# Cross-attention's query and output products as seven half-block products in place of eight, with the order of four engines written out

## The chip, the cores and the metric

The kernel runs on one core of one Trainium2 chip, in one launch. The metric is the device time in microseconds. The kernel before was run three times; every run also has a time of its own, and one more execution was profiled. Each execution gives the core's span (first to last instruction) and the clock that TensorE was granted, as a share of full speed.

## The reference

A block of a diffusion transformer, all in float32, for 8 batches of 512 rows of width 512, with 16 heads of width 32. `ctx` has 77 rows a batch. Cut to what matters:

```python
# phase x: cross-attention with a modulated layer norm
q = (ada_ln(x) @ Wq + bq)                       # 8 x 512 x 512
k, v = split(ada_ln(ctx) @ Wkv + bkv)           # 8 x 77 x 512 each
x = x + softmax(q k^T / sqrt(32)) v @ Wp + bp   # per head
# phase a: self-attention, gated
x = x + gate_a * (self_attention(modulate(ln(x))) @ W_proj + b_proj)
# phase c: cross-attention with a plain layer norm
q_c = ln(x) @ W_qc + b_qc
k_c, v_c = split(ln(ctx) @ W_kvc + b_kvc)
x = x + softmax(q_c k_c^T / sqrt(32)) v_c @ W_cproj + b_cproj
# phase m: MLP, gated
x = x + gate_m * (gelu(modulate(ln(x)) @ W_mlp1 + b_mlp1) @ W_mlp2 + b_mlp2)
```

## The kernel before

The kernel goes through the phases x, a, c and m one after the other; x between phases lies in DRAM, and a batch of it (four tiles of 128 x 512) is loaded into one of three buffers. `cross_phase` does phases x and c; it is the part that changes.

In `cross_phase` a unit is one batch `b` and one group `fc` of four heads (128 columns of q), 32 units a phase. For a unit:

- `queries(b, fc)` makes q transposed, 128 x 512, from four matmuls over the 128-row blocks of the transposed, normalised x (`mm_T`, line 353); ScalarE takes it out of PSUM with bias and scale (`qT`, line 579).
- `scores(b, fc)` makes 16 small matmuls of 77 columns (line 597) into two PSUM tiles of two heads each (`sc[0]`, `sc[1]`, pool `ps_s`). VectorE takes row maxima (line 606) and subtracts them (608), ScalarE takes the exp of the 128 x 616 block (611), VectorE sums (613), takes reciprocals (614) and multiplies (615). So it does for both tiles.
- `outputs(b, fc, ps)` turns the weights of each of the four heads with four transposes (634); ScalarE copies each turned head out (`pT`, 635); four matmuls against the values follow (639), and VectorE adds a bias (`oT`, 646).
- `project(b, t)` makes one 128 x 512 block of the output projection from four matmuls (`mm_N`, 361); VectorE adds the bias row (`res`, 376), GpSimd adds x (380), and SyncE's queue stores it (381).
- `ln_T` takes the statistics of a batch on VectorE (276, 277), a reciprocal square root by an integer seed and three Newton steps of small operations (288 to 297), normalises (`xh`, 301), and turns the result with 16 transposes (339); ScalarE copies them out (`xnT`).

TensorE alone has a written order in these phases (`manual_schedule(engines={ENG.PE})`); the other engines' orders come from the scheduler. `Filler` is a queue of generators: between the four turns of one unit, `fill.pump()` issues one matmul each of the next unit's query; what is left (the projection of the batch before, layer-norm transposes) is issued by `fill.drain()`. Softmax of a unit runs on VectorE and ScalarE while TensorE turns and multiplies for the unit before it.

PSUM has in these phases two double tiles for scores, two banks with the tag `m` (queries, projection, `o_ps`) and two with the tag `t` (turned heads, layer-norm transposes).

In phase x, `later_modulation(b)` follows a batch's last projection and makes one of six modulation blocks, whose weights it loads itself (`mod_unit`). In phase c, the keys of the last two head groups are put into the `Filler` first (`head`).

The MLP of phase m already uses seven products for eight half blocks (`Quad`, matmuls at line 1214, VectorE additions at 1222, one ScalarE copy at 1229, GELU at 1247).

Of the kernel before, what the change touches and what calls it, by code (L numbers as in the profile page):

```python
# [10 lines left out]
F32 = mybir.dt.float32  # L11
I32 = mybir.dt.int32
AF = mybir.ActivationFunctionType
ALU = mybir.AluOpType
# [11 lines left out]


class Filler:

    def __init__(self):
        self.q = deque()
        self.done = set()
        self.credit = 0.0
        self.left = 0
        self.rate = 0.0

    def add(self, key, gen, n=4):
        self.q.append((key, gen))  # L40
        self.left += n

    def pace(self, slots):

        self.rate = self.left / slots

    def step(self):
        while self.q:
            key, gen = self.q[0]
            try:  # L50
                next(gen)
                self.left -= 1
                return True
            except StopIteration:
                self.done.add(key)
                self.q.popleft()
        return False

    def pump(self):
        self.credit += self.rate  # L60
        while self.credit >= 1.0:
            self.credit -= 1.0
            if not self.step():
                self.credit = 0.0
                return

    def need(self, key):
        while key not in self.done:
            assert self.q, key
            if not self.step():  # L70
                break
        assert key in self.done, key

    def drain(self):
        while self.step():
            pass
# [3 lines left out]
def tile_pixart_block(ctx: ExitStack, tc: tile.TileContext, a: dict, out: bass.AP):  # L80
# [55 lines left out]
    def mod_unit(wname, bname, u, dst, psp, tag, gate=None, plus_one=False):  # L136


        w = load_w(wname, u)
        ps = psp.tile([P, H], F32, tag=tag, name=f"mod_ps_{wname}_{u}")  # L140
        if gate is not None:
            for k in range(KC):
                nc.tensor.matmul(
                    ps[:B, :], lhsT=csT[:, k, :], rhs=w[:, k, :],
                    start=(k == 0), stop=(k == KC - 1),
                )
            b_row = load_row(bname, u, "bv", parts=B)
            nc.vector.tensor_tensor(b_row, ps[:B, :], b_row, ALU.add)
            nc.sync.dma_start(out=gate, in_=b_row)
            return  # L150
# [76 lines left out]
    with tc.tile_pool(name="setup_ps", bufs=2, space=PSUM) as spp:  # L227
# [22 lines left out]
        for name in ("L0_xcond_bq", "L1_xcond_b_qkv", "L1_xcond_b_qc"):  # L250
# [66 lines left out]
    def ln_T(b, eps, nm, pool, psp, res, scale=None, shift=None, bufs=5, tag="t"):  # L317
# [6 lines left out]
        yield  # L324
        mv, y = run(pieces)
        xh = pool.tile([P, NT, H], F32, tag="xh", bufs=1, name=f"xh_{nm}{b}")
        if nm == "c" and b == 0:

# [3 lines left out]
        else:  # L332
            for t in range(NT):
                normalise(xh[:, t, :], xb[:, t, :], mv, y, t, P)
        yield
        for k in range(KC):
# [3 lines left out]
            o = pool.tile([P, N], F32, tag="xnT", bufs=bufs, name=f"xnT_{nm}{b}_{k}")  # L340
            if scale is None:
                nc.scalar.copy(o, pt)
            else:
                nc.scalar.activation(
                    o, pt, AF.Identity, bias=shift[:, k, b : b + 1], scale=scale[:, k, b : b + 1]
                )
            res.append(o)
# [24 lines left out]

    def add_residual(b, t, ps, b_row, gate, pool, nm):

        tmp = pool.tile([P, H], F32, tag="res", bufs=2, name=f"res_{nm}{b}_{t}")
        nc.vector.tensor_tensor(tmp, ps, b_row, ALU.add)  # L376
        xt = x_sb[nm, b][:, t, :]
        if gate is not None:
            nc.gpsimd.tensor_tensor(tmp, tmp, gate, ALU.mult)
        nc.gpsimd.tensor_tensor(xt, xt, tmp, ALU.add)  # L380
        nc.sync.dma_start(out=x_dst[nm][b][ts(t, P), :], in_=xt)
# [33 lines left out]
    with tc.tile_pool(name="ps_s", bufs=2, space=PSUM, reuse_waits="tile") as ps_s:  # L415
# [17 lines left out]
        def context_x(eps, w_k, w_v, bkv, work, prep, cx):  # L433
# [38 lines left out]
            for j in range(KC):  # L472
                for g in range(2):
                    pk = ps_m.tile([P, H], F32, tag="m", name=f"ckT_ps_x{j}_{g}")
                    for k in range(KC):
# [5 lines left out]
                        kT[:, j, ts(g, HB)], pk[:, :HB], AF.Identity, bias=bias_cols(bkv, 1, j)  # L481
# [4 lines left out]
        class ContextC:  # L486
# [62 lines left out]
            def keys(self, j):  # L549
                for at, n, cT in ((0, H, self.cT), (H, RL, self.last)):  # L550
                    pk = ps_m.tile([P, H], F32, tag="m", name=f"ckT_ps_c{j}_{at}")
                    for k in range(KC):
# [7 lines left out]
                        bias=bias_cols(self.bkv, 1, j),  # L560
                    )
                return evac

        def cross_phase(
# [3 lines left out]

            w_q, w_o = w
            bq, bkv, bo_row = names  # L570
            work = stack.enter_context(tc.tile_pool(name=f"work_{nm}", bufs=2, reuse_waits="tile"))
            fill = Filler()
            st = [dict(xT=[], q={}, o=[]) for _ in range(B)]

            def queries(b, fc):
                pq = ps_m.tile([P, H], F32, tag="m", name=f"q_ps_{nm}{b}_{fc}")
                yield from mm_T(pq, w_q, fc, st[b]["xT"])
                qT = work.tile([P, N], F32, tag="qT", bufs=2, name=f"qT_{nm}{b}_{fc}")
                nc.scalar.activation(
                    qT, pq, AF.Identity, bias=bias_cols(bq, 1, fc), scale=SCALE  # L580
                )
                st[b]["q"][fc] = qT

            def project(b, t):
                pr = ps_m.tile([P, H], F32, tag="m", name=f"proj_ps_{nm}{b}_{t}")
                yield from mm_N(pr, w_o, st[b]["o"], ts(t, P))
                add_residual(b, t, pr, bo_row, None, work, nm)
                if t == NT - 1 and between is not None:
                    between(b)

            def scores(b, fc):
                nmf = f"{nm}{b}_{fc}"
                qT = st[b]["q"].pop(fc)
                sc = [ps_s.tile([P, 2, H], F32, tag="s", name=f"s_{nmf}_{i}") for i in range(2)]
                for t in range(NT):
# [808 lines left out]
```

## Time and profile before

| what | value |
|---|---|
| runs | 2602.67 us median of 3 (2601.11 to 2604.31) |
| profiled execution | 2603.28 us, span 2601.4 us, granted clock 0.989 |
| phase x, from the first query (75.4 to 488.3 us) | 412.9 us, TensorE busy 405.1, VectorE 287.2, ScalarE 156.6, GpSimd 40.6 |
| phase a (530 to 1340 us) | 810.0 us, TensorE 752.1, VectorE 658.8, ScalarE 565.6, GpSimd 589.6 |
| phase c, from the first query (1405.1 to 1790.5 us) | 385.4 us, TensorE 381.1, VectorE 286.8, ScalarE 150.8, GpSimd 40.0 |
| phase m (1793 to 2601 us) | 808.0 us, TensorE 792.2, VectorE 442.6, ScalarE 143.9, GpSimd 128.7 |

In what follows, a row of groups by form reads: line, engine, operation, output from inputs, shape, count, then busy time in all, mean length of one in ns, and the idle time of the engine just before them with what ended it. A row of the timeline reads: start, length (both in us), engine, line, operation, count. A row of windows reads: stretch, length, busy time (and count) of TensorE, TensorE's weight loads, VectorE, ScalarE and GpSimd, then the granted clock, the share of DMA time and GB/s. Matmuls overlap, and a float32 matmul has two records of which the second starts before the first ends.

### The profile page before, as it was taken

What the parts mean: (1) busy time and instruction counts of PE and PEld (TensorE: products, weight loads), DVE (VectorE), ACT (ScalarE), POOL (GpSimd) and SP (SyncE); (2) the same over time, 40 slices, a digit from 0 to 9 for tenths busy, and PEclk for the clock granted to TensorE, in tenths of its full rate; (3) what the DMA queues carried; (4) which work ended last, traced back from release to release, by engine and by line L of the source; (5) the groups of instructions that cost most, each with busy time, mean ns of one, the idle gap of its engine ahead of it and who ended that gap; (6) DMA issues with size and microseconds to landing.
All of it is one profiled execution on the core that took longest, in us unless ns stands there. A gap on an engine that the chain in (4) does not pass through costs nothing.

```text
span 2601.4 us, 32647 instructions
## 1 busy us (share of the span) xinstructions
PE 2488.0 (96%) x12517; PEld 1425.3 (55%) x12517; DVE 1744.8 (67%) x3109; ACT 1074.6 (41%) x1471; POOL 848.0 (33%) x692
## 2 busy tenths in 40 slices
PE   7999999989999999999979999998999999999998
PEld 3555554423333333333324555555888888888887
DVE  3676667478787887887784877777655555555553
ACT  1433334366776766767653433432221221221220
POOL 1000000156877768678662011114012012012021
PEclk9999999989999999999989999999999999999999
DMA  7111121279999999999986011113001011011010
GB/s 256 38 54 53 63 72 58 81 147 200 186 195 194 183 194 186 193 203 186 200 180 225 13 57 37 42 53 122 25 30 53 21 33 53 19 35 53 17 37 25
DMA packets 116407, 264.90 MB, mean 102 GB/s; under 512 B 12595, under 2 KB 29059, under 8 KB 116251
## 3 DMA queue, kind: packets, MB, share of 16 engines
q0 software_dynamic: 37152, 134.28, 27.6%
q1 hardware_dynamic: 73157, 116.76, 13.5%
q10 hardware_dynamic: 5941, 11.76, 1.2%
q8 instruction: 99, 1.62, 0.2%
q14 instruction: 58, 0.47, 0.1%
HBM read 226.39 MB, written 36.37 MB: 101 GB/s over the span
## 4 chain that ended last, share of the span: by engine, by line
PE 40%; issue 27%; DMA 12%; DVE 12%; POOL 6%; ACT 2%; POOLq 0%; SPq 0%; ACTq 0%; DVEq 0%
DMA e_a<-mxd_a 9%; PE proj_ps_c L361 4%; PE proj_ps_x L361 4%; PE q_ps_c L353 4%; PE q_ps_x L353 4%; DVE mx_a L836 3%; PE pT_ps_c L634 2%; PE v_ps L361 2%; PE pT_ps_x L634 2%; POOL res_m L1313 2%; PE proj_ps_a L361 2%; DVE sum_a L886 2%; DVE tu_a L847 2%; POOL xr L1314 2%; DVE part_a L848 2%
## 5 line engine op out<-in xcount | busy, mean ns | idle before, releaser
L879 ACT ACTIVATE e_a<-e_a 128x1024 f32<-128x1024 f32 x256 | 262.4, 1056 | 99.4 <-DMA e_a<-mxd_a 98.9
L870 POOL DMA_DIRECT2D e_a<-mxd_a x256 | 248.0, 2049 | 142.7 <-DMA mxd_a<-mxT_a 130.3
L834 ACT COPY e_a<-sT_a 128x1024 f32<-128x1024 f32 x256 | 253.0, 1010 | 91.3 <-DVE mx_a L836 66.0
L1313 POOL TENSOR_TENSOR res_m<-res_m,gate_m 128x256 f32<-128x256 f32 x64 | 52.1, 814 | 665.9 <-DVE res_m L1311 665.9
L1247 ACT ACTIVATE hT<-hT,bcol 128x512 f32<-128x512 f32 x128 | 92.0, 722 | 237.3 <-DVE hT L1222 229.2
L886 POOL TENSOR_TENSOR sum_a<-e_a,e_a 128x1024 f32<-128x1024 f32 x64 | 150.1, 2363 | 121.8 <-ACT e_a L879 121.3
L380 POOL TENSOR_TENSOR x_x<-x_x,res_x 128x512 f32<-128x512 f32 x32 | 40.6, 1270 | 409.9 <-DVE res_x L376 343.1
L886 POOL TENSOR_TENSOR sum_a<-sum_a,e_a 128x1024 f32<-128x1024 f32 x64 | 171.1, 2684 | 2.7 <-ACT e_a L879 2.7
L816 PE MATMUL sT_a<-qT_a,kT_a 32*128 32x512 f32 x1024 | 153.2, 647 | 18.5 <-ACT e_a L834 16.7
L836 DVE TENSOR_TENSOR mx_a<-sT_a,mx_a 128x1024 f32<-128x1024 f32 x128 | 150.3, 1215 | 23.3 <-PE sT_a L816 23.3
L896 PE MATMUL o_ps_a<-e_a,v 128*32 128x512 f32 x1024 | 145.0, 618 | 13.3 <-ACT e_a L879 13.3
L380 POOL TENSOR_TENSOR x_c<-x_c,res_c 128x512 f32<-128x512 f32 x32 | 40.6, 1269 | 346.4 <-DVE res_c L376 289.5
L635 ACT COPY pT_x<-pT_ps_x 77x512 f32<-77x512 f32 x128 | 72.7, 577 | 189.4 <-PE pT_ps_x L634 189.4
L635 ACT COPY pT_c<-pT_ps_c 77x512 f32<-77x512 f32 x128 | 72.7, 577 | 163.4 <-PE pT_ps_c L634 163.4
L353 PE MATMUL q_ps_x<-xnT_x,w_L_xcond_Wq 128*128 128x512 f32 x256 | 132.7, 604 | 0.0
L1214 PE MATMUL q_ps_h<-x_m,w_L_xcond_W_mlp 128*128 128x256 f32 x512 | 131.7, 380 | 0.0
L1214 PE MATMUL q_ps_h<-xT_m,w_L_xcond_W_mlp 128*128 128x256 f32 x512 | 131.4, 379 | 0.0
L914 DVE RECIPROCAL rz_a<-z_ps_a 128x512 f32<-128x512 f32 x32 | 107.4, 3358 | 34.0 <-PE z_ps_a L907 34.0
L353 PE MATMUL q_ps_c<-xnT_c,w_L_xcond_W_qc 128*128 128x512 f32 x256 | 130.1, 594 | 0.0
L836 DVE TENSOR_TENSOR mx_a<-sT_a,e_a 128x1024 f32<-128x1024 f32 x64 | 77.8, 1224 | 77.0 <-PE sT_a L816 39.3
L1214 PE MATMUL q_ps_h<-x_m,w_s 128*128 128x256 f32 x512 | 122.8, 383 | 5.9 <-DVE w_s L1168 4.9
L361 PE MATMUL proj_ps_a<-w_L_xcond_W_proj,oT_a 128*128 128x512 f32 x256 | 117.6, 604 | 9.9 <-ACT xnT_a L739 9.9
(249 smaller groups left out, 5133.0 us busy)
## 6 DMA issues: line engine op xcount, KB each, us to landing
e_a<-mxd_a POOLq DMA_DIRECT2D x256, 512.0 KB, 11.4
xa<-x_x SPq DMA_DIRECT2D x32, 256.0 KB, 2.0
xr_a<-xa SPq DMA_DIRECT2D x32, 256.0 KB, 4.7
xc<-xr_a SPq DMA_DIRECT2D x32, 256.0 KB, 8.3
x_c<-xc SPq DMA_DIRECT2D x8, 1024.0 KB, 7.1
w_L_xcond_W_mlp<-in_L_xcond_W_mlp_dram SPq DMA_DIRECT2D x8, 1024.0 KB, 6.1
xm<-x_c SPq DMA_DIRECT2D x32, 256.0 KB, 2.0
x_m<-xm SPq DMA_DIRECT2D x8, 1024.0 KB, 5.3
```

The source lines that it names most:

```text
L353: nc.tensor.matmul(ps, lhsT=w[:, k, ts(j, P)], rhs=xT[k], start=(k == 0), stop=(k == KC - 1))
L361: nc.tensor.matmul(ps, lhsT=xT[k][:, cols], rhs=w[:, k, :], start=(k == 0), stop=(k == KC - 1))
L635: nc.scalar.copy(pTs[-1][:, h % 2, :], pp[:S, :])
L816: nc.tensor.matmul(sc[h // 2][:, h % 2, :], lhsT=kT[ts(h, HD), ts(k, P)], rhs=qT[ts(h, HD), :], start=True, stop=True,)
L834: nc.scalar.copy(self.e[k][i], sc[i])
L836: nc.vector.tensor_tensor(self.mx[1 - i], sc[1 - i], self.e[0][1 - i] if k == 1 else self.mx[1 - i], ALU.max,)
L870: nc.gpsimd.dma_start(out=self.e[k][i].rearrange("p h n -> p (h n)"), in_=self.mxd[2 * i : 2 * i + 2, :] .rearrange("h n -> (h n)").partit ...
L879: nc.scalar.activation(self.e[k][i], self.e[k][i], AF.Exp)
L886: engine.tensor_tensor(sum_i, self.e[0][i] if k == 1 else sum_i, self.e[k][i], ALU.add)
L896: nc.tensor.matmul(self.po[ts(h, HD), :], lhsT=vt[:, self.fc * P + h * HD : self.fc * P + (h + 1) * HD], rhs=self.e[k][h // 2][:, h % 2, : ...
L914: nc.vector.reciprocal(r, self.pz)
L1214: nc.tensor.matmul(self.banks[n][:, half], lhsT=lhsT, rhs=rhs, start=(k == 0), stop=(k == len(pairs) - 1),)
```

## The change

Queries and the output projection of a batch are 512 x 512 x 512 products. They are now made of quadrants of 256 by the scheme with seven products (that of the MLP) in place of eight. A `Seven` makes half of the columns of all seven products: two 128 x 256 output blocks in each half, so two `Seven`s for a batch's queries and two for its projection. Each of its steps issues one product (two matmuls of 256 columns) and what reads it. Two products share a PSUM bank of tag `m`.

```diff
+        class Seven:
+            ORDER = (1, 2, 6, 7, 5, 4, 3)
+            def steps(self):
+                for n, i in enumerate(self.ORDER):
+                    if n % 2 == 0:
+                        bank = ps_m.tile([P, 2, N2], F32, tag="m", name=f"s{n}_ps_{self.nm}")
+                    ps = bank[:, n % 2]
+                    for k in range(2):
+                        nc.tensor.matmul(
+                            ps, lhsT=self.lhs[i][:, k], rhs=self.rhs[i][:, k],
+                            start=(k == 0), stop=(k == 1),
+                        )
+                    if i == 1:
+                        p1 = self.temp("p1")
+                        self.first(p1, ps)
+                    elif i == 2:
+                        nc.vector.tensor_tensor(self.dst[0, 0], ps, p1, add)
+                    elif i == 6:
+                        u2 = self.temp("u2")
+                        nc.vector.tensor_tensor(u2, ps, p1, add)
+                    elif i == 7:
+                        u3 = self.temp("u3")
+                        self.third(u3, ps, u2)
+                    elif i == 5:
+                        p5 = self.temp("p5")
+                        self.fifth(p5, ps)
+                        nc.gpsimd.tensor_tensor(u2, u2, p5, add)
+                        nc.gpsimd.tensor_tensor(self.dst[1, 1], u3, p5, add)
+                    elif i == 4:
+                        nc.vector.tensor_tensor(self.dst[1, 0], ps, u3, add)
...
+                    else:
+                        nc.vector.tensor_tensor(self.dst[0, 1], ps, u2, add)
...
+                    yield
```

For queries `first` is a ScalarE activation with the bias, for the projection a VectorE addition of the bias row; `fifth` is a ScalarE copy (with one more GpSimd addition for the projection). The sums of half blocks that the scheme needs are four 128 x 512 operations: `sq` and `to` of the weights once a phase, `x_sums` of x a batch (on GpSimd; on VectorE for batch 0), `o_sums` of the attention output a batch (on GpSimd; on VectorE for the last).

The loop over units now writes the order of TensorE, VectorE, ScalarE and GpSimd (`ALL_BUT_SYNC`); `Filler` is gone. In the first gaps of the diff stand `turn` and `keep` of heads 2 and 3, in the last one pieces of the layer norm's statistics, `o_sums`, `x_sums`, `next_x` and `between`. `now` is the unit whose scores are made, `before` the one whose weights are turned; `g` is a `Seven`, `turned` the layer-norm transposes of the next batch:

```diff
+                if fc == 0:
+                    g = queries(b, 1)
+                elif fc == 3 and more:
+                    g = queries(b + 1, 0)
+                elif fc in (1, 2) and b > 0:
+                    g = project(b - 1, fc - 1)
+                if fc == 2 and more:
+                    turned = ln[b + 1]
+                now = Softmax(b, fc)
+                now.scores()
+                if before:
+                    before.turn(0)
+                    before.keep(0)
+                now.exp(0)
+                next(g, None)
+                next(turned, None)
+                next(g, None)
+                if before:
+                    before.turn(1)
+                    before.keep(1)
+                next(g, None)
+                next(turned, None)
+                now.exp(1, 0)
+                now.total(0)
...
+                next(g, None)
+                next(turned, None)
+                now.divide(0)
...
+                next(g, None)
+                next(turned, None)
+                now.exp(1, 1)
+                if before:
+                    before.outputs()
+                now.total(1)
+                next(g, None)
+                last = now.divide(1)
+                next(g, None)
...
```

`scores` now issues both reductions and the subtraction for the first tile only. The second tile stays in PSUM, and its exp is taken from there in eight activations of 77 columns with the negated maximum as bias:

```diff
+                def exp(self, i, r=0):
+                    if i == 0:
+                        nc.scalar.activation(self.p[0], self.p[0], AF.Exp)
+                        return
+                    for t in range(NT):
+                        nc.scalar.activation(
+                            self.p[i][:, r, t, :], self.sv[i][:, r, t, :], AF.Exp,
+                            bias=self.mx[i][:, r, t : t + 1],
+                        )
```

Further edits: `oT`'s bias addition and, but for batch 0 of phase x, the layer norm's normalising move from VectorE to ScalarE; `o_ps` moves from tag `m` to `t`; the scale moves from q to the keys; statistics of the batch after next are taken at the end of fc 3 and of fc 0, the reciprocal square root and the normalising at the end of fc 1; the x of a batch is loaded at fc 2; the keys of `head` are made before the first query; modulation weights are loaded one block ahead and the block stands after fc 2 (`Modulation`); after the last unit both `Seven`s of the last projection follow its outputs. Phase a, phase m and the setup keep their code.

## The prediction

> **What bounds the kernel now.** I read the page first, then the busy times of the two cross-attention phases, then one group of heads on TensorE in order of time, then the durations by form.
>
> ```profile
> PE 2488.0 (96%) x12517; PEld 1425.3 (55%) x12517; DVE 1744.8 (67%) x3109; ACT 1074.6 (41%) x1471; POOL 848.0 (33%) x692
> ```
> ```profile
> 75.40:488.30 412.90, 405.09 (x2575) 216.01 (x2573) 287.16 (x578) 156.57 (x257) 40.62 (x32) 0.98 0.17 57
> 1405.10:1790.50 385.40, 381.08 (x2451) 198.77 (x2450) 286.76 (x575) 150.82 (x258) 40.02 (x32) 1.00 0.17 58
> ```
> TensorE is busy for 405 of 413 us and 381 of 385 us; every other engine has slack. So fewer TensorE passes would be worth their full time, as long as nothing makes TensorE wait. One group on it (start, length):
>
> ```profile
> 1753.97 1.13 PE L597 MATMUL s_c<-ckT_c,qT_c 32*128 32x77 f32 x32
> 1755.04 0.66 PE L634 MATMUL pT_ps_c<-ident,p_c 128*77 128x128 f32 x4
> 1755.53 1.02 PE L353 MATMUL q_ps_c<-xnT_c,w_L_xcond_W_qc 128*128 128x512 f32 x2
> ...
> 1760.38 1.06 PE L639 MATMUL o_ps_c<-pT_c,cv_c 77*32 77x512 f32 x8
> 1761.38 3.70 PE L361 MATMUL proj_ps_c<-w_L_xcond_W_cproj,oT_c 128*128 128x512 f32 x8
> 1765.01 1.13 PE L597 MATMUL s_c<-ckT_c,qT_c 32*128 32x77 f32 x32
> ```
> The period is 11.04 us without a hole. With the layer norm's 16 transposes a batch takes 47.2 us (scores at 1508.25 to scores at 1555.41). The durations that the chain below uses:
>
> ```profile
> L606 DVE TENSOR_REDUCE mx_c<-s_c 128x8 f32<-128x616 f32 x64 | 48.1, 793 | 32.5 <-PE s_c L597 32.5
> L608 DVE TENSOR_TENSOR p_c<-s_c,mx_c 128x616 f32<-128x616 f32 x64 | 47.9, 790 | 0.0
> L1222 DVE TENSOR_TENSOR hT<-q_ps_h,u_h 128x256 f32<-128x256 f32 x192 | 81.4, 424 | 37.5 <-PE q_ps_h L1214 29.2
> L611 ACT ACTIVATE p_c<-p_c 128x616 f32<-128x616 f32 x64 | 43.6, 713 | 11.4 <-DVE p_c L608 11.3
> L1229 ACT COPY p_h<-q_ps_h 128x256 f32<-128x256 f32 x64 | 23.7, 371 | 183.6 <-PE q_ps_h L1214 183.6
> L558 ACT ACTIVATE ckT_c<-ckT_ps_c,bcol 128x104 f32<-128x104 f32 x4 | 1.4, 347 | 0.9 <-PE ckT_ps_c L553 0.9
> L313 ACT ACTIVATE xh_c<-x_c,off,lny_c 128x512 f32<-128x512 f32 x4 | 2.9, 802 | 7.2 <-DVE off L308 7.2
> ```
>
> **What TensorE saves.** Per batch, queries and projection are now 32 matmuls of 512 columns at 0.855 us (two records, 0.427 us apart). They become four `Seven`s of seven products. A product is four records of a 256-column pass; in the MLP, which already works so, the next product starts 0.86 us later and the last result is there after 1.03 us. A group with a `Seven` costs 1.06 scores + 4 x 0.44 turns + 7 x 0.86 + 1.0 outputs + 0.3 at the joints = 10.15 us against 11.04: 0.89 us less, some 52 us over the 58 such groups (29 in each phase). **So all waiting that the new order brings must stay below 0.89 us a group.**
>
> **The waits it brings.** All engines but SyncE now run in the written order. In the built program the second product of each bank waits for the reader of the first: product 2 for `p1`, 7 for `u2`, 4 for `p5`. In the kernel before, TensorE waits for nothing inside a query (idle before L353: 0.0). In the MLP the pair goes out first and is read afterwards (idle before L1214 mostly 0.0), so that row gives these waits a price of nothing. [...]
>
> And `p1` of a query stands on ScalarE behind `exp(0)`, which waits for VectorE's subtraction; behind product 2 stand, on TensorE, three turns, the other products and the outputs. From the first reduction, a group's chain is: reduction 0.75 + subtraction 0.79 + exp 0.66 + `p1` 0.47 (between the 256- and 512-wide rows, 0.37 and 0.69) = 2.67; product 2, a turn, product 6: 0.86 + 0.44 + 1.03 = 2.33; `u2` 0.42; product 7, a turn, product 5: 2.33; `p5` 0.37; four 77-column exps; sum 0.75, result 21 0.40, reciprocal and division 1.0, result 12 0.42: 2.57; nine handovers of 0.03. The exps are in no row: four of 104 columns give 1.39, half of the whole exp 0.36. I take 1.0, near the first (0.32 + 3 x 0.22, since their rows overlap by 0.1). Sum: **11.9 us**. TensorE idles 1.5 to 2.2 us of it at product 2. In a project group `p1` is VectorE's, behind the second reduction: the same within 0.1.
>
> What is added between one group's last result and the next reduction:
> - Query groups (fc 3 and 0): the next scores need the last result for their second half (0.65 us), and two layer-norm statistics (2 x 0.70) come first on VectorE: +1.4. Both following groups: 13.3.
> - After fc 1: the rsqrt chain, 13 small operations 0.195 apart, 2.5 us. ScalarE then normalises in 2.9 us (4 x 0.70, the 0.80 us rows), *ahead of* the `keep` that the next group's turns need. TensorE comes to the first layer-norm transpose at 1.2 us after fc 1's last result and gets the data at 5.4: a hole of 4 us. From there ScalarE's list sets the pace (four keeps, five exps, four copies, `p5`: 7.3 us of rows and 1.7 of waits for turns), then 2.6 us on VectorE: 16.8 us.
> - After fc 2 nothing: 11.9.
>
> **Batch: 13.3 + 13.3 + 16.8 + 11.9 = 55.3 us, against 47.2.**
>
> Moved work that I take as hidden: the sums on GpSimd (8 x 1.27) and its small additions fill 24 of 55 us; the first sum that product 6 needs is ready 0.2 us ahead, in fc 3, so if GpSimd is late each us costs one. `oT` on ScalarE follows the exps and is read a group later. Stores and the next x on SyncE's queue: the store ends about 33 us into the batch, the load takes 7.1 (row of x_c<-xc), and the statistics want it near 42: 1.4 us to spare. Modulation weights are now loaded a block ahead; its 3.5 us of TensorE work remain, now with every engine behind them.
>
> **Ends of a phase.** The first query alone waits for its own evacuations: 8.6 us against 4.3. Batch 0 has no projections, but its chains still run: 11.6 + 12.1 + 11.9 + 11.9 = 47.5. Keys 2 and 3 (9.0 us, 1410.58 to 1419.54), which filled holes, now stand alone. The last batch: 12.5 + 14.7 (four statistics) + 14.4 (rsqrt, no normalise) + 7.2 (no `Seven`), then turns, outputs, `o_sums` on VectorE (3.4 us, with `p1` behind them) and two `Seven`s in a row: 21.8. Together 70.6.
>
> Phase c: 9.0 + 8.6 + 47.5 + 6 x 55.3 + 70.6 = 467.5, against 385.4: +82. Phase x: 8.6 + 47.5 + 3.5 + 5 x (55.3 + 4.0) + 55.8 + 70.6 = 482.5, against 411 (75.4 to the last projection's end at 486.3): +71. (4.0 is the modulation block and 0.5 for the wider evacuation of xnT.) The other phases keep their code. Profiled execution: 2603.3 us, of it 2601.4 span, 0.6 us over the median of 2602.67. 2603 + 153 = 2756, say **2755 us**.
>
> **Bounds.** Exps at 0.36: -0.64 x 58 = -37; at 1.39: +23. The 4 us hole half hidden: -35, wholly -70. Each TensorE stall may cost 0.1 for the weight load before its matmul (L353's load starts 0.11 ahead): +20. VectorE operations with two SBUF inputs may be held by GpSimd, as the 128x512 row of L1348 (0.95 us, against 0.69 at L1339) suggests: 8 x 0.26 x 16 = +33, taken as zero since the chain has slack beside the divisions. TensorE's clock: 0.66 in 520 to 530 us, busy 6.95, yet 0.98 in 1810 to 1820, busy 7.02; only a long single hole lowers it. If each hole of 4 us cost 3.4 us (0.34 of that slice) it would be 14 x 3.4 = +48; I take none, as ScalarE paces that stretch. [...]
>
> **Rivals.**
> 1. *TensorE stays the bound, and it is faster.* For it: 98% busy, and the MLP runs such products without holes. It needs `p1` before TensorE ends product 1, that is under 0.89 us of waiting a group. Then -52, plus about 10 for the bare ends: 2560. Against: exp cannot start before scores, reduction and subtraction, 2.6 us into the group, when TensorE is through product 1 at 2.4.
> 2. *The layer norm's hole closes* (statistics early, ScalarE catches up): 13.3 + 13.3 + 11.9 + 1.8 + 11.9 = 52.2, and the ends as above: 3.1 x 14 less, about 2710; with short exps 2675.
> 3. *Worse*: clock, GpSimd and weight loads together: 2830.
> 4. *It does not do what it says*: out, the built program has 14 half-width matmuls where 8 full ones stood.
>
> **How the numbers follow.** My forecast 0.64 (own range 2710 to 2800), rival 2 0.18, rival 3 0.05, rival 1 0.10, and 0.03 for a balance within 0.2%, 5 us, which is about what a measurement of this kernel can tell. The range goes from 2650 (short exps and half the hole) to 2820.
>
> **What would show it.** Right: on TensorE, idle time before the products ended by ACT `p1` and DVE `u2`, about 2 us and 0.2 us a group; a hole of 3 to 5 us before each lnT; group periods of 12 to 13 and one near 17; TensorE busy near 80% in both phases; exp rows of 0.3 us; the phases near 480 and 465 us. Wrong: group periods under 11, or idle at product 2 under 0.5 us, would mean that the chain from scores to `p1` runs ahead of TensorE.

## The result, and the profile after

The changed kernel takes 2851.82 us (median of 4 runs, 2848.57 to 2856.67), the kernel before on the same chip 2601.89 us (2600.09 to 2604.31): a ratio of 1.0961, 95% interval 1.0942 to 1.0981. The direction of the forecast held; the size did not. 2755 us with a range up to 2820 was predicted, so 97 us were missed, and the time lies 32 us outside the range.

The page of the kernel after, the line of busy times; then the two cross-attention phases, x from 80.0 us (first scores) to the first layer-norm transpose of phase a, c from its first layer-norm transpose to the first MLP product:

```profile
PE 2547.5 (89%) x13285; PEld 1616.9 (57%) x13285; DVE 1799.9 (63%) x3239; ACT 1226.8 (43%) x2079; POOL 1145.6 (40%) x982
```
```profile
80.00:610.90 530.90, 432.08 (x2934) 311.99 (x2933) 309.33 (x646) 229.60 (x556) 180.43 (x171) 0.90 0.12 42
1526.40:2041.30 514.90, 410.49 (x2866) 293.64 (x2865) 314.34 (x643) 229.74 (x567) 191.95 (x180) 0.93 0.11 39
```

Between the same marks the kernel before needs 406.3 and 391.3 us. That is 124.6 and 123.6 us more, 248 of the 250.3 by which the span grew; phases a and m are as long as before within 3 us. TensorE's share fell to 81% and 80%, near the 80% predicted, but that is luck: its busy time did not fall with the work. It rose from 399.8 and 385.5 us to 432.1 and 410.5, at a granted clock of 0.90 and 0.93 in place of 0.98 and 1.00.

One batch of phase c by its four groups, fc 3, 0, 1 and 2, in windows from scores to scores:

```profile
1705.27:1717.98 12.71, 10.97 (x85) 7.87 (x84) 7.77 (x15) 6.08 (x16) 9.45 (x8) 1.00 0.37 125
1717.98:1731.46 13.48, 10.99 (x86) 7.93 (x85) 9.07 (x19) 6.00 (x16) 2.28 (x3) 1.00 0.00 0
1731.46:1746.70 15.24, 12.44 (x86) 9.15 (x85) 9.80 (x20) 5.72 (x15) 6.72 (x8) 0.89 0.00 1
1746.70:1766.53 19.83, 15.54 (x102) 11.31 (x101) 11.36 (x29) 10.45 (x23) 5.15 (x6) 0.83 0.07 28
```

Together 61.26 us, where 55.3 were predicted and 47.16 are needed before (the six full batches of this phase take 59.4 to 61.3 us). The two groups that are furthest off are the two whose clock fell. What TensorE does in them, in order of time:

```profile
1732.92 0.68 PE L705 MATMUL s_c<-ckT_c,qT_c 32*128 32x77 f32 x16 [0.77 <-DVE qT_c L552]
...
1737.08 1.13 PE L527 MATMUL s_ps_oc<-w_L_xcond_W_cproj,oT_c 128*128 128x256 f32 x4 [2.02 <-DVE p_oc L688]
1738.05 0.66 PE L757 MATMUL pT_ps_c<-ident,p_c 128*77 128x128 f32 x4
1738.50 1.92 PE L527 MATMUL s_ps_oc<-to_c,os_c 128*128 128x256 f32 x4
...
1752.62 0.47 PE L286 MATMUL lnT_ps_c<-ident,xh_c 128*128 128x128 f32 x1 [3.33 <-ACT xh_c L260]
...
1755.01 1.92 PE L527 MATMUL s_ps_oc<-w_L_xcond_W_cproj,oT_c 128*128 128x256 f32 x4
```

The holes are the predicted ones (2.02 us at product 2, 3.33 and three times 0.23 before the layer-norm transposes). Behind each the reader sees what was not predicted: products of four records that take 1.92 us instead of 1.03 to 1.13. The four largest waits of TensorE in phase c (us in total, times, longest); `s_ps_qc` and `s_ps_oc` are products of a query and of a projection, `p_qc` and `p_oc` here their `p1`, `lnT_ps_c` the layer norm's transposes:

```profile
PE s_ps_qc L527 <- ACT p_qc L649: 27.1, 16, 2.5
PE lnT_ps_c L286 <- ACT xh_c L260: 27.1, 28, 3.3
PE s_ps_oc L527 <- DVE p_oc L688: 24.1, 10, 5.1
PE s_c L705 <- DVE qT_c L552: 8.3, 15, 0.8
```

And why the hole before the transposes is as long as it is: VectorE at the end of fc 1, in the first operations of the reciprocal square root ("the root" below), beside GpSimd's two residual additions (the POOL row, 2.97 us for two):

```profile
1747.56 0.90 DVE L235 TENSOR_SCALAR lnv_c<-mv_c 128x4 f32<-128x4 f32 x1
1748.50 1.18 DVE L237 TENSOR_SCALAR lny_c<-lnv_c 128x4 int32<-128x4 int32 x1
1749.72 0.17 DVE L240 TENSOR_SCALAR lnv_c<-lnv_c 128x4 f32<-128x4 f32 x1
```
```profile
1746.68 2.97 POOL L683 TENSOR_TENSOR x_c<-x_c,res_c 128x512 f32<-128x512 f32 x2
```

Two operations on four columns take 0.90 and 1.18 us until GpSimd is through, the next like them 0.17.

### The profile page after: what moved, and what is told of

It reads as the page before. It is cut to its first block, busy times and chain, and to the rows that moved or that the text cites. A ratio compares the mean times of both kernels' runs of the same rounds, so it can differ in the third digit from the quotient of the medians.

```text
span 2851.7 us, 35619 instructions
## 1 busy us (share of the span) xinstructions
PE 2547.5 (89%) x13285; PEld 1616.9 (57%) x13285; DVE 1799.9 (63%) x3239; ACT 1226.8 (43%) x2079; POOL 1145.6 (40%) x982
## 5 line engine op out<-in xcount | busy, mean ns | idle before, releaser
L990 PE MATMUL sT_a<-qT_a,kT_a 32*128 32x512 f32 x1024 | 152.5, 648 | 17.5 <-ACT e_a L1008 15.7
L1070 PE MATMUL o_ps_a<-e_a,v 128*32 128x512 f32 x1024 | 145.0, 621 | 13.4 <-ACT e_a L1053 13.3
L299 PE MATMUL q_ps_a<-xnT_a,w_L_xcond_W_qkv 128*128 128x512 f32 x256 | 124.1, 613 | 0.0
L307 PE MATMUL v_ps<-w_L_xcond_W_qkv,xnT_a 128*128 128x512 f32 x256 | 122.0, 621 | 0.0
L299 PE MATMUL k_ps_a<-xnT_a,w_L_xcond_W_qkv 128*128 128x512 f32 x256 | 120.4, 608 | 0.0
L1407 PE MATMUL q_ps_y<-w_L_xcond_W_mlp,h_s 128*128 128x256 f32 x512 | 113.1, 379 | 0.0
```

Source lines behind the costliest of these rows:

```text
L299: nc.tensor.matmul(ps, lhsT=w[:, k, ts(j, P)], rhs=xT[k], start=(k == 0), stop=(k == KC - 1))
L307: nc.tensor.matmul(ps, lhsT=xT[k][:, cols], rhs=w[:, k, :], start=(k == 0), stop=(k == KC - 1))
L990: nc.tensor.matmul(sc[h // 2][:, h % 2, :], lhsT=kT[ts(h, HD), ts(k, P)], rhs=qT[ts(h, HD), :], start=True, stop=True,)
L1070: nc.tensor.matmul(self.po[ts(h, HD), :], lhsT=vt[:, self.fc * P + h * HD : self.fc * P + (h + 1) * HD], rhs=self.e[k][h // 2][:, h % 2, : ...
L1407: nc.tensor.matmul(self.banks[n][:, half], lhsT=lhsT, rhs=rhs, start=(k == 0), stop=(k == len(pairs) - 1),)
```

## The experiments

Two theories stood. The first: the chain of waits was summed rightly, and the missing 97 us are the two costs that the prediction set to nothing, TensorE's clock after holes and GpSimd holding VectorE. The rival: the chain itself is longer than the sum, and clock and overlap only go along with it. A second question is what the order costs and what the seven products cost. All times, with one batch of phase c from each trace (the full batches of one run differ by up to 3.5 us):

| run | time, us | ratio to before (95%) | batch, us |
|---|---|---|---|
| before | 2601.9 to 2604.3 | 1 | 47.16 |
| after | 2851.8 | 1.0961 (1.0942 to 1.0981) | 61.26 |
| holes filled | 2821.6 | 1.0835 (1.0817 to 1.0853) | 57.92 |
| without GpSimd's work | 2798.4 | 1.0747 (1.0721 to 1.0772) | 58.45 |
| both | 2770.3 | 1.0638 (1.0620 to 1.0656) | 55.18 |
| eight products, new order | 2692.4 | 1.0342 (1.0324 to 1.0360) | 51.81 |
| the same, root early | 2616.4 | 1.0046 (1.0031 to 1.0061) | 46.39 |
| readers in pairs | 2785.0 | 1.0698 (1.0667 to 1.0729) | 57.91 |
| root early | 2824.6 | 1.0851 (1.0832 to 1.0869) | 58.13 |
| `p1` first | 2829.4 | 1.0858 (1.0839 to 1.0876) | 58.00 |
| five edits | 2690.4 | 1.0326 (1.0310 to 1.0341) | 51.13 |
| products reordered | 2668.2 | 1.0245 (1.0229 to 1.0260) | 48.74 |
| ends changed | 2669.4 | 1.0242 (1.0225 to 1.0259) | 48.46 |
| exp and division later | 2663.0 | 1.0227 (1.0208 to 1.0245) | 47.95 |

**Holes filled.** Idle products in TensorE's holes, 144 in the two phases:

```diff
+            def warm(tile, n):
+                for _ in range(n):
+                    nc.tensor.matmul(tile, lhsT=ident, rhs=w_q[:, 0, :], start=True, stop=True)
 # beside fc 0, 1 and 3, between products 1 and 2:
+                    before.room(1)
+                    warm(before.pp, 2)
 # ln_T, ahead of the first transposes:
+            if warm is not None and k == 0 and b > 0:
+                warm(pt, 4)
```

> The changed kernel with work added on TensorE and nothing else: two idle 128x512 products of some 0.86 us each ahead of product 2 beside the groups fc 0, 1 and 3, and four ahead of the first lnT transposes, written into the tile that the following transposes overwrite. Nothing waits for them and their results are used nowhere. Theory A (holes of 2 to 4 us lower the clock that TensorE is granted afterwards, and that is some 88 us of the changed kernel's 2852): the granted clock of the two cross phases rises from 0.90 and 0.93 to 0.97 or more, the products of 1.9 us go, and the time falls to 2760 to 2810. Theory B (the time is the length of the chain of waits, and the clock only follows): the time stays at 2850 or rises by up to 60 us, 22 groups by two phases with some 0.4 us each that do not fit the hole, 2845 to 2910.

Measured: 2821.6 us. TensorE was given more to do, and the kernel became 30 us faster. The groups fc 1 and fc 2 of one batch, and the product behind the hole:

```profile
1712.16:1726.08 13.92, 12.67 (x90) 8.69 (x89) 9.79 (x20) 5.65 (x15) 6.73 (x8) 1.00 0.01 1
1726.08:1743.88 17.80, 16.41 (x110) 11.15 (x109) 11.37 (x29) 10.46 (x23) 5.17 (x6) 1.00 0.08 30
```
```profile
1719.19 1.03 PE L529 MATMUL s_ps_oc<-to_c,os_c 128*128 128x256 f32 x4
```

The clock is 1.00 in both, the product takes 1.03 us, and the groups are 1.3 and 2.0 us shorter (15.24 and 19.83 in the changed kernel). Groups whose clock was full anyway are as long as before the filling (12.72 and 13.48). So the clock fell because of the holes, and that cost time; over the execution it is 0.981, where the changed kernel has 0.959. But it was 30 us and not the 40 to 90 expected, between the ranges of the two theories: in most groups the chain on the other engines sets the period, and a faster TensorE only waits longer.

**Without GpSimd's work.** The residual is not added and most sums are not made again:

```diff
-                    nc.gpsimd.tensor_tensor(xt, xt, res[t], add)
-                    nc.sync.dma_start(out=x_dst[nm][b][ts(t, P), :], in_=xt)
+                    nc.sync.dma_start(out=x_dst[nm][b][ts(t, P), :], in_=res[t])
 # x_sums (and o_sums likewise):
+                if b > 0:
+                    st[b]["t"] = st[0]["t"]
+                    return
```

> The changed kernel with most of GpSimd's work of the two phases left out: the residual is not added (the projection goes out alone), and the sums and differences are made for the first batch only and used again for the others. Theory A (GpSimd's transfers hold VectorE's small operations and divisions, which lie on the chain to the normalising): the root's operations fall from 0.90 and 1.18 us to 0.2 and 0.3, the divisions from 0.86 to 0.80, the lnT hole by 2 to 3 us a batch with a part of the clock: 2790 to 2825. Theory B (the overlap is a coincidence, or the chain does not feel it): 2840 to 2855.

Measured: 2798.4 us, 53 less. VectorE by form (line, operation, count, busy time, mean in ns):

```profile
L749 DVE TENSOR_TENSOR p_c<-p_c,sm_c 128x616 f32<-128x616 f32 x64 | 51.6, 807 | 2.2
L237 DVE TENSOR_SCALAR lny_c<-lnv_c 128x4 int32<-128x4 int32 x8 | 1.4, 170 | 0.3
L235 DVE TENSOR_SCALAR lnv_c<-mv_c 128x4 f32<-128x4 f32 x8 | 1.3, 161 | 0.0
```

In the changed kernel the same three have means of 858, 932 and 720 ns. The wait before the transposes falls from 27.1 to 17.4 us in phase c, with it the clock's loss (0.970 over the execution, against 0.959). The hold is shown. The 53 us hold more than it: the sums that product 6 of fc 3 waits for are gone too (fc 3 takes 12.20 us, 12.71 in the changed kernel).

**Both together.** The two edits above in one kernel, so again without the residual and with reused sums.

> The two edits of the first and the seventh run together: idle products in the holes, and most of GpSimd's work of the two phases left out (no residual, sums and differences of the first batch used throughout). This is the changed kernel with the two costs taken away that the prediction had set to nothing. Theory A (clock and GpSimd are what the prediction missed, and they add up): 30 and 53 us less than 2852, 2760 to 2785, near the predicted 2755. Theory B (they are the same loss seen twice): 2790 to 2805, what GpSimd's alone gave.

Measured: 2770.3 us, 81.5 less than after: 30.2 and 53.4 add up. The batch (fc 0 to fc 3):

```profile
1720.12:1733.59 13.47, 12.70 (x90) 8.69 (x89) 9.07 (x19) 6.00 (x16) 1.41 (x2) 1.00 0.01 1
1733.59:1746.99 13.40, 12.69 (x89) 8.68 (x88) 9.34 (x20) 5.64 (x15) 2.14 (x3) 1.00 0.00 1
1746.99:1763.03 16.04, 15.78 (x110) 11.13 (x109) 9.62 (x29) 10.45 (x23) 2.14 (x3) 1.00 0.30 99
1763.03:1775.30 12.27, 12.19 (x90) 8.67 (x89) 7.78 (x15) 6.00 (x16) 1.41 (x2) 1.00 0.12 45
```

55.18 us, group by group beside the predicted 13.3, 13.3, 16.8 and 11.9; that the sum meets 55.3 so closely is in part luck, since fc 2 is 0.8 us under its forecast and the other three are up to 0.4 over. With the two costs away, the batches of phase c are those that the prediction described, and there the rival falls. Phase x stays longer than its sum, as told below.

**Eight products in the new order.** Each half is two plain blocks, each from four matmuls of 512 columns, with no sums:

```diff
+                for fc in (j, j + 2):
+                    pq = ps_m.tile([P, H], F32, tag="m", name=f"q_ps_{nm}{b}_{fc}")
+                    for k in range(KC):
+                        nc.tensor.matmul(
+                            pq, lhsT=w_q[:, k, ts(fc, P)], rhs=xT[:, k, :],
+                            start=(k == 0), stop=(k == KC - 1),
+                        )
...
+                    nc.scalar.activation(qT, pq, AF.Identity, bias=bias_cols(bq, 1, fc))
```

> The order of the changed kernel with the multiplication of before: each half is two 512 column products of four accumulated steps, read once by ScalarE (queries) or VectorE (projection); no sums or differences on GpSimd or VectorE, all other edits kept. Theory A (the seven products' own waits and GpSimd's work cost most of the 250 us): some 11.0 us of TensorE a group and a hole of 2 to 4 us a batch, 2625 to 2700. Theory B (the order is what costs, a chain of 12 us a group with the exponentials in eight pieces): 2760 to 2850.

Measured: 2692.4 us. That is 88 us over the kernel before, for the order, and 159 us under the changed kernel, for the seven products. Three groups take 11.03 us, as before; all that the order loses in a batch is in fc 2:

```profile
1635.94:1654.65 18.71, 15.13 (x90) 8.24 (x89) 10.49 (x24) 10.09 (x22) 2.53 (x2) 0.91 0.08 29
sum 51.81, PE 48.23 PEld 25.05 DVE 33.97 ACT 28.81 POOL 5.06; mean PE 12.06 PEld 6.26 DVE 8.49 ACT 7.20 POOL 1.26
```

**The same with the root early.** In `ln_T` a step ends behind the reciprocal root, and the loop makes it behind the first division of fc 1; the normalising stays at that group's end.

```diff
         mv, y = run(pieces)
+        off = None if (nm, b) == ("x", 0) else offsets(mv, y, NT)
+        yield
         xh = pool.tile([P, NT, H], F32, tag="xh", bufs=1, name=f"xh_{nm}{b}")
...
                 now.divide(0)
+                if more and fc == 1:
+                    next(ln[b + 1])
```

> The order alone with eight products, and the reciprocal root in the middle of fc 1. In the order alone three groups took 11.03 us and that of fc 2 18.7, where before had 13.5. Theory A (the late normalising is all that the order costs in the steady part): fc 2 falls from 18.7 to 13.5 us, 14 times 5.2 us less: 2610 to 2630. Rival (the exponentials in pieces or the transposes' own chain hold fc 2 as well): 2650 to 2690.

Measured: 2616.4 us; 76 of the order's 88 us were the late root, which the normalising waits for.

```profile
1627.38:1640.67 13.29, 13.00 (x90) 7.33 (x89) 9.38 (x15) 10.09 (x22) 2.53 (x2) 1.00 0.11 41
sum 46.39, PE 46.10 PEld 24.15 DVE 32.80 ACT 28.93 POOL 5.06; mean PE 11.53 PEld 6.04 DVE 8.20 ACT 7.23 POOL 1.26
```

The written order is then as good as the scheduler's inside a batch (46.39 against 47.16); what is left, 12 us, lies outside these batches: the head of phase c alone, from its first transpose to its first scores, takes 22.9 us, where the kernel before, which makes keys 2 and 3 behind its first scores, took 7.3.

**Root early, with the seven products.** The same diff on the changed kernel.

> The changed kernel with the twelve small operations of the reciprocal root moved from the end of fc 1 to its middle (behind the first division), the normalising on ScalarE left at the end of fc 1, where it now finds its scales ready. Theory A (the hole ahead of the lnT transposes, 27.1 us in phase c, closes, and the clock of 0.83 in fc 2 returns with it): 2760 to 2790. Theory B (the hole alone): 2790 to 2810. Rival C (ScalarE's four tiles, not the root, are what the transposes wait for, so that the exponentials of fc 2 are late instead): 2835 to 2860.

Measured: 2824.6 us, 27 less, not the 42 to 92 of the two theories, and outside the rival's range too. TensorE's waits in phase c:

```profile
PE lnT_ps_c L287 <- ACT xh_c L260: 2.3, 6, 0.4
...
PE s_ps_oc L528 <- DVE p_oc L689: 40.4, 16, 5.1
```

The hole before the transposes is gone (27.1 to 2.3 us), and 16 us of it come back at product 2 of the projections, whose `p1` on VectorE is now what is late. The root in the middle of fc 1 is held there too: one of its multiplications has a mean of 432 ns, 201 in the changed kernel. It also shows that the split of 88 and 159 us holds for the late root only: with the root early in both, the order costs 12 us and the seven products 208 (2824.6 against 2616.4).

**Readers in pairs.** Both products of a bank are issued before what reads them:

```diff
-                    if i == 1:
-                        p1 = self.temp("p1")
-                        self.first(p1, ps)
...
+                    held.append((i, ps))
+                    if n % 2 == 1 or n == 6:
+                        for at in held:
+                            read(*at)
+                        held = []
```

> The changed kernel with the readers of each bank emitted after both of its products, so that product 2 (and 7, and 4) no longer waits for the reader of the product beside it in the bank; the order on TensorE is the same. Theory A (the waits for p1, u2 and p5 make holes, and these lower the clock too): the waits of 27.1 + 24.1 + 8.3 us in phase c and about as much in phase x go, and the clock of fc 0, 1 and 3 returns to 1.0: 2690 to 2760. Theory B (holes cost their length alone): 2852 less 100 to 120, but less what the chain takes back, 2740 to 2790. Rival C (the wait moves: the next pair's bank or the scores wait for the same late readers): 2820 to 2860.

Measured: 2785.0 us, 67 less, in theory B's range; the clock of the execution stayed at 0.960. The waits at products 2, 7 and 4 are gone altogether, and fc 0 and fc 1 fall to 11.28 us. Part of them came back elsewhere:

```profile
PE lnT_ps_c L286 <- ACT xh_c L260: 35.4, 28, 4.9
...
PE s_ps_qc L556 <- POOL xs_c L592: 22.3, 6, 3.7
...
PE s_c L715 <- DVE qT_c L545: 13.4, 16, 1.5
```

The transposes' wait grew from 27.1 us, GpSimd's differences (1.1 us in the changed kernel) now hold up product 6 of fc 3, and the scores wait 0.84 us for the last half of q, which VectorE adds behind a division.

**`p1` first.** One line moved:

```diff
-                now.exp(0)
                 next(g, None)
+                now.exp(0)
                 next(turned, None)
```

> The changed kernel with one line moved: product 1 and its reader come ahead of the first exponential, so that on ScalarE p1 of the queries no longer stands behind an operation that waits for VectorE. TensorE's order is the same. Theory A (the place behind the exponential is what the product 2 of the queries waits for): the waits of 27.1 and 22.7 us for the queries' p1 fall below 10 each, the projections' (on VectorE, behind the maxima) stay: 2790 to 2820. Theory B (the exponentials' own chain sets the group, 12.7 us remain): 2840 to 2855.

Measured: 2829.4 us, between the two ranges. The queries' waits for `p1` fall from 27.1 and 22.7 us to 9.0 each, and fc 0 from 13.48 to 11.94 us: the place behind the exponential was the cause there, as the prediction had it. fc 3 stays at 12.72:

```profile
1750.22 1.13 PE L527 MATMUL s_ps_qc<-xnT_c,w_L_xcond_W_qc 128*128 128x256 f32 x4 [0.56 <-ACT p_qc L649]
...
1752.79 1.13 PE L527 MATMUL s_ps_qc<-xs_c,sq_c 128*128 128x256 f32 x4 [1.00 <-POOL xs_c L582]
```

What product 2 no longer waits, product 6 waits for GpSimd's differences.

**Five edits together.** Pairs and the early root, and three more:

```diff
-                last = now.divide(1)
-                next(g, None)
+                next(g, None)
+                last = now.divide(1)
 # x_sums: two differences on VectorE, two on GpSimd
-                engine.tensor_tensor(t3, b22, b12, sub)
+                other.tensor_tensor(t3, b22, b12, sub)
 # statistics: both pieces at fc 3
+                    next(ln[b + 2])
```

> The changed kernel with readers in pairs and the reciprocal root in the middle of fc 1 as in the two experiments before, and three more edits of order: the second division of a group goes behind the reader of product 3 (the next scores waited 0.84 us for that reader, which stood behind the division on VectorE), both pieces of the statistics go to fc 3, and of the four differences of the normalised columns VectorE makes two and GpSimd two (product 6 in fc 3 waited 3.7 us for GpSimd's). Theory A (with the waits gone TensorE's own 10.4 us set the group, at full clock): three groups of 10.4 to 10.7 and one of 12.5 to 14 a batch, 44 to 46 us against 47 before, the longer ends of both phases stay: 2590 to 2640. Rival (VectorE, with some 12 us of work in fc 1, or the late differences become the bound): a batch of 50 to 54 us, 2680 to 2740.

Measured: 2690.4 us, 50 over theory A's range and in the rival's. The batch is 51.13 us at full clock, with VectorE busy for 39.67 of it, so it is not VectorE's work alone: TensorE's two largest waits in phase c are for ScalarE's copies of turned heads (26.3 us) and for VectorE's differences (13.1 us). These two differences in fc 3, beside GpSimd's residual additions:

```profile
1694.88 1.76 DVE L593 TENSOR_TENSOR xs_c<-xnT_c 128x512 f32<-128x512 f32 x1
1696.67 1.63 DVE L594 TENSOR_TENSOR xs_c<-xnT_c,xs_c 128x512 f32<-128x512 f32 x1
```

**Products reordered** (the ninth run, in what follows; the one above is the fifth). The order 1, 2, 6, 5, 7, 3, 4, with `u2 + p5` in a tile of its own, one piece of statistics at fc 3 and one at fc 0 again, and VectorE's differences in fc 2:

```diff
-            ORDER = (1, 2, 6, 7, 5, 4, 3)
+            ORDER = (1, 2, 6, 5, 7, 3, 4)
-                        nc.gpsimd.tensor_tensor(u2, u2, p5, add)
+                        nc.gpsimd.tensor_tensor(u4, u2, p5, add)
```

> Seven products, readers in pairs, root in the middle of fc 1, second division last, as before; the products in the order 1, 2, 6, 5, 7, 3, 4, so that the half of the query that the next scores need is ready one product earlier; the statistics back in their two places; the differences on VectorE in its idle time of fc 2, away from GpSimd's additions. Theory A (TensorE's own work sets three groups at 10.4 to 10.6 us and fc 2 at 12.7 to 13.3): a batch of 44 to 45 us, 5 fewer in each of 14 than the 51.1 of the fifth run: 2590 to 2620. Rival (VectorE's and ScalarE's chain still holds 11 us or more): 2635 to 2680.

Measured: 2668.2 us, in the rival's range. The batch is 48.74 us: fc 3 at last runs without a wait, in 10.41 us; fc 0 and 1 take 12, fc 2 14.3. The largest wait left is for ScalarE's copies of turned heads (23.2 us in phase c).

```profile
1632.01:1642.42 10.41, 10.41 (x85) 8.01 (x84) 8.33 (x17) 5.86 (x16) 6.15 (x6) 1.00 0.29 94
```

Around the end of fc 1, VectorE beside GpSimd:

```profile
1668.57 1.89 DVE L761 TENSOR_TENSOR p_c<-p_c,sm_c 128x616 f32<-128x616 f32 x1
1670.38 0.79 DVE L738 TENSOR_REDUCE mx_c<-s_c 128x8 f32<-128x616 f32 x1
1671.20 0.80 DVE L739 TENSOR_TENSOR p_c<-s_c,mx_c 128x616 f32<-128x616 f32 x1
```
```profile
1668.53 3.06 POOL L700 TENSOR_TENSOR x_c<-x_c,res_c 128x512 f32<-128x512 f32 x2
```

The division, with both inputs in SBUF, takes 1.89 us; the two passes over the scores in PSUM behind it, of which one lies in the same 3.06 us, take 0.79 and 0.80 us, as in the kernel before (means of 793 and 790 ns).

**Ends changed.** Keys beside the groups of batch 0, and a plain last projection:

```diff
+                elif fc in (1, 2) and head:
+                    g = head[fc - 1]
...
+            for t in range(NT):
+                project_plain(B - 1, t)
```

> The same with the ends changed: keys 2 and 3 of phase c beside the groups fc 1 and 2 of batch 0, which have no projection, and the last batch's projection as sixteen plain 512 column matmuls without sums. Theory A (the bare ends cost what they are long): 8 to 9 us for the keys and 2 to 5 for each tail less than the ninth run: 2570 to 2605. Rival (the groups of batch 0 become longer by the keys' time, and the plain products cost the tails what the sums saved): within 5 us of the ninth run.

Measured: 2669.4 us, within the spread of the run before it. The rival's range held: the groups with the keys, fc 1 and fc 2 of batch 0, took 13.46 and 14.07 us in place of 11.91 and 10.21, more than the head of the phase gained (15.7 us from the first transpose to the first scores, 17.9 before this edit).

**Exponential and division later.** The ninth kernel with two orders changed:

```diff
                 now.scores()
+                    last = before.divide(1)
+                    statistics(*before.at)
...
-                now.exp(0)
 # behind the copy of the second turn:
+                now.exp(0)
```

> The ninth run's kernel with two orders changed: the first exponential goes behind the copy of the second turn (turns 3 waited for that copy, which stood behind the exponential, and that behind VectorE's statistics and divisions), and a group's second division and the statistics go behind the next group's three passes over the scores, which read PSUM and were not held by GpSimd (0.79 and 0.80 us beside the residual additions, where the division took 1.74 and 1.89). Theory A (TensorE's 10.4 us then set three groups of four, 12.7 to 13.3 the one with the transposes): 44 to 45 us a batch against 48.6 in the ninth run, 2605 to 2625. Rival (the root, still beside GpSimd, or ScalarE's normalising ahead of the first turn's copy keep fc 2 above 14 us, and the groups before it at 12): 2645 to 2670.

Measured: 2663.0 us, 5 less than the ninth run, which is not clear of noise (1.0208 to 1.0245 against 1.0229 to 1.0260). The time lies in the rival's range, but not for its reason: fc 2 takes 13.08 us, as theory A had it, and the other three 11.28, 11.30 and 12.29, where theory A had 10.4. The sum line of the four groups' windows:

```profile
sum 47.95, PE 46.05 PEld 33.51 DVE 39.66 ACT 27.92 POOL 21.52; mean PE 11.51 PEld 8.38 DVE 9.91 ACT 6.98 POOL 5.38
```

At full clock in all four groups the batch is still 0.8 us longer than before, with VectorE busy for 39.7 us of it (36.5 before). The batch is no longer where most of the loss lies, though. Phase c is 27.7 us longer than before (419.0 against 391.3 us), and 21.6 of these stand at its ends: 10.7 from the first transpose to the first scores, 10.9 from the first scores of the last batch but one to the first MLP product. No version with seven products beat the kernel before; the best with the new order, eight products, is 0.46% slower (0.31 to 0.61).

## Why the prediction was right or wrong

**Direction and chain: right.** In the batch shown, product 2 idled 1.37 to 2.1 us (1.5 to 2.2 predicted), product 7 0.17 (0.2), the hole before the transposes was 3.33 and 0.7 (4), the short exps had a mean of 331 ns and four of them 0.96 us (1.0). Shown by the run with both edits: 55.18 us a batch against the sum of 55.3, and in phase c 473.7 us against 391.3 before, +82.4 where +82 was predicted. The terms given for the group behind fc 1 add up to 17.0 and not 16.8; it took 16.04. That the waits at the second product of each bank stay, where the MLP's row gave them a price of nothing, no row of the kernel before showed; after, those at product 2 alone came to 27.1 and 24.1 us in phase c, and they went when the readers came in pairs. The rival *TensorE stays the bound* fell on the test that the prediction named.

**The step that failed: two terms set to nothing in the bounds.**

- *TensorE's clock*, "I take none, as ScalarE paces that stretch", and "only a long single hole lowers it". It measured 30 us by the filling. The two slices beside the second quote do not bear it out: in the kernel before, the holes that end in 520 to 530 us are 0.78 and 2.69 us long (clock 0.66), those that end in 1810 to 1820 us 2.81 and 2.11 (clock 0.98). In the changed kernel products at 1.92 us also came behind holes of 2.10 us (fc 0, with one of 0.32 ahead of it) and 2.02 (fc 1, with one of 0.77), and in fc 1 and fc 2 TensorE's slower products are on the path: with the holes filled these groups were 1.3 and 2.0 us shorter. The trace shows that the outcome is not fixed by the group. In fc 0 of one batch of phase c, and of the next:

```profile
1662.11 1.13 PE L527 MATMUL s_ps_qc<-xnT_c,w_L_xcond_W_qc 128*128 128x256 f32 x4 [2.10 <-ACT p_qc L649]
...
1663.65 1.92 PE L527 MATMUL s_ps_qc<-xs_c,sq_c 128*128 128x256 f32 x4
```
```profile
1723.22 1.13 PE L527 MATMUL s_ps_qc<-xnT_c,w_L_xcond_W_qc 128*128 128x256 f32 x4 [2.10 <-ACT p_qc L649]
...
1724.63 1.03 PE L527 MATMUL s_ps_qc<-xs_c,sq_c 128*128 128x256 f32 x4
```

  Behind the same hole of 2.10 us product 6 takes 1.92 us in one batch and 1.03 in the next, where fc 1 has the slow one. A group that is hit takes 14.82 us (fc 0) or 15.24 (fc 1), one that is not 13.48 or 13.92. No hole in the fc 0 shown was longer than 2.1 us. Why one batch is hit in fc 0 and the next in fc 1, no run here shows.
- *GpSimd holding VectorE*, "+33, taken as zero since the chain has slack beside the divisions". With GpSimd's work away it was 53 us, the waits for its sums among them. The slack beside the divisions was not whole: in fc 1 a division beside GpSimd's sums took 1.25 us, and the scores waited 0.77 us for the last half of q, which VectorE adds behind it; with both edits that wait was 0.32. And the hold fell on the root as well, thirteen operations that the prediction priced at 0.195 us each, at the one place where nothing covers them: the two held there took 2.08 us together. In the ninth run a division, with both inputs in SBUF, took 1.89 us beside GpSimd's additions, and the passes over the scores in PSUM behind it 0.79 and 0.80. The root's two held operations have one input each, so the two inputs that the prediction named are not needed for a hold; what decides it, no run here shows.

The two make 81.5 of the 97 us. Of the other 15, about 11 lie in phase x: with both edits it takes 488.4 us between the marks that were 406.3 apart, +82 against the predicted +71. Its five full batches with a modulation block take 58.9 to 61.2 us, where 59.3 were predicted: 4 of the 11. About 2 each lie at the first query, in batch 0 and behind the first scores of the last batch. What makes them longer was not tried, and the last 4 of the 15 us were not placed.

**The saving was smaller than said.** 10.15 us of TensorE a group was predicted; the ninth run's fc 3, without a wait, takes 10.41. The 0.86 us from product to product holds in the middle; the last two start 0.97 and 0.95 us before what follows. So 0.62 us a group were to be had, not 0.89.

**The range.** Rival 3, clock and GpSimd and weight loads together at 2830 us with a chance of 0.05, comes nearest to what was measured; no run shows its part for the weight loads. Beside +33 and +20 its number leaves 22 us for the clock, a term that no run shows; the filling measured 30 us. With the +48 of the bounds for the clock the sum is 2856, and with +48 and +33 alone 2836, so the end of 2820 lay below a sum that stood in the text. The lower end does not follow from the bounds either: short exps and half the hole give 2755 - 37 - 35 = 2683, and 2650 needs the whole hole. That +48 and +33 make 81, where the two edits gave 81.5, is luck: the clock was 30 and GpSimd 53. The two costs hardly overlap, since 30.2 and 53.4 add up to 83.6; but they come from the same place in part, as the wait before the transposes fell from 27.1 to 17.4 us without GpSimd's work and the clock of the execution rose with it, from 0.959 to 0.970.

## What to carry to other kernels

A change that saves an engine work pays only if that engine stays without holes: here 0.6 us a group of saving met 1.7 to 4.3 us of idle time on TensorE, and each wait that was taken away uncovered another one (`p1`, GpSimd's sums, the last half of q, the turn's copy) without end in twelve runs. Sum the chain of the other engines between two uses of the one that is to gain, and give the clock after a hole and the hold by GpSimd a price wherever a row shows them. Where a change moves both order and arithmetic, run one without the other first: that comparison put 159 us on the seven products and 88 on the order, and the next run put 76 of these 88 on the late root alone.

## What was not expected of the hardware

- Idle products sped the kernel up: 144 products more on TensorE, 30 us less. Repeated holes of 2.0 to 2.1 us were enough for products at 1.92 us in place of 1.03, in some batches and not in others.
- An operation on 128 x 4 elements took 1.18 us beside GpSimd's additions of 128 x 512, and a mean of 0.17 without. So the hold cost it far more than its own length: it was the second of two held operations, and it ended where GpSimd's pair of additions did (1749.68 and 1749.65 us).
